# Feed-forward weight centred, scaled and summed on GpSimd beside the first softmax in a gated cross-attention block

## The chip, the cores and the metric

The kernel runs on one core of a Trainium2 chip. A core has five engines, each with an instruction queue that is worked off in order: TensorE (PE; its weight loads are listed as PEld), VectorE (DVE), ScalarE (ACT), GpSimd (POOL) and SyncE (SP, which here only issues DMA transfers). The metric is the device time of one execution in microseconds (us), the median over several runs.

## What is computed

Four sequences of 2048 tokens with 512 features attend to 77 context vectors with 16 heads, and pass through a feed-forward layer that is one matrix out of eight. Both branches are gated by the tanh of a scalar:

```python
q = split_heads(layernorm(x) @ Wq)
k, v = split_heads(context @ Wk), split_heads(context @ Wv)
attn = softmax(einsum('bhid,bhjd->bhij', q, k) * SCALE)
x = x + tanh(g_xattn) * (merge(einsum('bhij,bhjd->bhid', attn, v)) @ Wo + bo)
idx = argmax(log_softmax(logits) + gumbel(u))
x = x + tanh(g_ffn) * (layernorm(x) @ W[idx] + b[idx])
```

All of it is in fp32.

## The kernel before

**Tiling.** The 8192 tokens are worked off in 16 groups of 512. Weights are folded first: `m` holds `Wq` and the keys of one sequence in one matrix, `vo` holds values times `Wo` times the gate, `wf` holds the chosen feed-forward matrix, centred over its input features and times its gate `tgf`. A group is then three products: scores (`ps_s`, weight `m`), attention (`ps_a`, weight `vo`) and feed-forward (`ps_f`, weight `wf`).

**Seven products in place of eight.** Every product of 2x2 blocks is done with seven block products (class `Seven`, lines 440 to 491). It needs sums of blocks on both sides: `weight_sum(w, n)` (L119) forms the weight's, four of them, into blocks 5, 3, 4 and 6 of a tile with 7 blocks; `Columns.sum` (L429) forms `T1` to `T4` of the tokens, in the tile `tq`. In `ORDER` (L442) step `s` multiplies one block and accumulates it in one of three PSUM banks; `post(s)` (L477) takes the result out. Steps 0, 1, 2 and 6 are copies on ACT (L467), steps 3, 4 and 5 additions on VectorE (L486). Step 2 accumulates further in the bank of step 0, so its matmuls wait until `post(0)` has copied that bank; step 4 waits so for `post(2)`, step 6 for `post(4)`.

**Order.** The order on every engine is that of the program text, written out by hand; nothing reorders it. An instruction waits for the semaphores of what it reads or overwrites. PSUM is one pool of 7 banks, taken in turn.

**The start of the kernel,** where the change lies:

- Weights are folded on TensorE (`project_k`, `project_v`, `build_m`). `kT`, the keys, lies in the first 2560 columns of the tile `wf`, and the last of the values, `vT[7]`, in columns 2560 to 2879 (L256); both are done with before `wf` gets its own contents there. `build_vo(p)` (L322) multiplies a pair of heads' values with `Wo`, with two evictions for each third of the keys on VectorE (`D`) or ACT (`A`), and stores the result to DRAM; `load_vo` loads it back.
- The scores of group 0 come in three parts: `s0` and `s1` with two pairs of heads' rows each, `s2` with one (L669, L683, L712). While `s0` runs, `gather` (L242) fetches the rows of the feed-forward weight to the tile `wfr` by indirect DMA, and GpSimd adds its four pieces (`sum_wf`, L629) into `wf`'s first 512 columns.
- While `s1` runs (L684 to L709), VectorE takes the statistics of group 1 in four steps of four (`n1.stats`, L698). At step 4 `centre_wf` (L635) lets TensorE form the mean of the weight in PSUM (a matmul with `ones`), and VectorE subtracts it from the four pieces. At step 5 ACT gathers group 1's statistics with eight small copies (`n1.gather`, L374, placed as `norm_step(n1, 0)`), and `scale_wf` (L641) has ACT multiply by `tgf` and write `wf`'s blocks 0 to 3 in eight operations.
- While `s2` runs, VectorE computes group 1's variance (`n1.calc`, L376) and GpSimd raises it to the power -1/2 (L393, `n1.power`).
- Then the scores of group 1 run on TensorE, with `build_vo(4)` to `build_vo(7)` between their steps, beside the first softmax: `head_max` on VectorE, `exps` on ACT, `head_sum` on VectorE, `head_scale` (L542) on GpSimd, `p_columns` (the transposes to `pT`, L546) on VectorE.
- `weight_sum(wf, 0)` stands between the third and fourth `head_scale` of group 0, and `weight_sum(wf, 1..3)` in the first attention (L868 to L872). The first feed-forward follows at L911.

Of the kernel before, what the change touches and what calls it, by code (L numbers as in the profile page):

```python
# [10 lines left out]
AF = mybir.ActivationFunctionType  # L11
ALU = mybir.AluOpType
# [7 lines left out]
def flamingo_block_kernel(  # L20
# [33 lines left out]
    nc = tc.nc  # L54
    NT, D = x.shape
# [7 lines left out]
    NP = H // 2  # L63
# [6 lines left out]
    BP = B * JP  # L70
    NDC = D // P
# [16 lines left out]
    def bank(name):  # L88
        return pm.tile([P, 512], F32, tag="mm", name=name)
# [6 lines left out]
    BLK = {(0, 0): 0, (0, 1): 1, (1, 1): 2, (1, 0): 3}  # L96
    m = cp.tile([P, 7, 2, KH, P], F32, tag="m")
    vo = cp.tile([P, 7, KH, D // 2], F32, tag="vo")
    wf = cp.tile([P, 7, 2, D // 2], F32, tag="wf")
# [14 lines left out]
    def flat(t):  # L114
        n = len(t.shape) - 1
        names = " ".join("abcdef"[:n])
        return t.rearrange(f"p {names} -> p ({names})")

    def weight_sum(w, n, engine=None):  # L119

        to, a, b_, op = ((5, 0, 3, ALU.subtract), (3, 3, 2, ALU.add), (4, 3, 0, ALU.subtract),
                         (6, 1, 4, ALU.subtract))[n]
        (engine or nc.gpsimd).tensor_tensor(flat(w[:, to]), flat(w[:, a]), flat(w[:, b_]), op)  # L123

    m_f, vo_f, wf_f = flat(m), flat(vo), flat(wf)
# [17 lines left out]
    t = wp.tile([P, NK * T + KH * T2], F32, tag="pT", name="wq")  # L143
    wq_f = t[:, : NP * D]
    wq = wq_f.rearrange("p (n f) -> p n f", n=NP)
    vT_f = t[:, NP * D :]
    xg, ys, ts_ = {}, {}, {}
# [17 lines left out]
    for _ in range(3):  # L165
        ps = bank("ps_w")
# [22 lines left out]
    def by_chunk(t):  # L189

        return t.rearrange("p (a q e) -> p q a e", a=NA, e=32)

    def chunked(t):
        return t.rearrange("p (q a e) -> p q a e", a=NA, e=32)
# [3 lines left out]
    tgx, tgf = tg[:, 0:1], tg[:, 1:2]  # L198
# [43 lines left out]
    def gather():  # L242
        t = row_tile("wfr").rearrange("p g j -> p (g j)").rearrange("p (c d) -> p c d", c=NDC)
        for c in range(NDC):
            at = bass.IndirectOffsetOnAxis(ap=rows_u[:, c : c + 1], axis=0)
            nc.gpsimd.indirect_dma_start(out=t[:, c, :], out_offset=None, in_=W, in_offset=at)
        at = bass.IndirectOffsetOnAxis(ap=rows_u[:, NDC:], axis=0)
        nc.gpsimd.indirect_dma_start(out=bf_r, out_offset=None,
                                     in_=b.rearrange("o (a j) -> (o a) j", j=P), in_offset=at)
        nc.gpsimd.tensor_scalar(bo_c, bo_c, tgx, None, ALU.mult)  # L250
        nc.gpsimd.tensor_scalar(bf_r, bf_r, tgf, None, ALU.mult)
        return t


    kT = wf_f[:, : NP * BP].rearrange("p (n b k r) -> p n b k r", n=NP, b=B, r=R)
    vT = [(vT_f[:, ts(p, BP)] if p < 7 else wf_f[:, ds(NP * BP, BP)]).rearrange(  # L256
        "p (r b k) -> p r b k", b=B, r=R) for p in range(NP)]

    kT_f = kT.rearrange("p n b k r -> p n b (k r)")
# [252 lines left out]
    def s_rows(i, k, cols):  # L512
        if i not in sc:
            sc[i] = wp.tile([P, HA, NG, JP], F32, tag="s", name="s")
        nc.vector.transpose(key_chunk(sc[i], k), cols.rearrange("p (g h r) -> p g h r", h=HA, r=R))  # L515
# [6 lines left out]
    def head_max(i, h):  # L522
        mx = stat[:, ds((16 + h) * NG, NG)]
        nc.vector.tensor_reduce(mx, head(i, h), AX.X, ALU.max)  # L524
        nmx[h] = small.tile([P, NG], F32, tag=f"nmx{h}", name="nmx")
        nc.vector.tensor_tensor(nmx[h], mx, norms[i].down, ALU.mult)  # L526
# [102 lines left out]
    def sum_wf(wfr):  # L629
        t = wf_f[:, :D]  # L630
        nc.gpsimd.tensor_tensor(t, wfr[:, 0, :], wfr[:, 1, :], ALU.add)
        nc.gpsimd.tensor_tensor(t, t, wfr[:, 2, :], ALU.add)
        nc.gpsimd.tensor_tensor(t, t, wfr[:, 3, :], ALU.add)

    def centre_wf(wfr):  # L635
        ps = bank("ps_w")
        nc.tensor.matmul(ps, ones, wf_f[:, :D], start=True, stop=True)
        for c in range(NDC):
            nc.vector.tensor_tensor(wfr[:, c, :], wfr[:, c, :], ps, ALU.subtract)

    def scale_wf(wfr):  # L641
        for c in range(NDC):
            for o in range(2):
                nc.scalar.activation(chunked(wf[:, BLK[o, c // 2], c % 2, :]),  # L644
                                     by_chunk(wfr[:, c, :])[:, ts(o, 2)], AF.Copy, scale=tgf)

    def scores0(i):
        return Seven("ps_s", w_scores, xc[i], (0, 1), SNAP)
# [7 lines left out]
    def norm_step(n, s):  # L656
        if s == 0:
            n.gather()
        elif s == 1:
            n.calc()  # L660
            n.power()
        elif s == 2:
            n.back()
# [6 lines left out]
    for s in range(6):  # L670
        s0.product(s)
        if s == 0:
            gates2()
            wfr = gather()
# [9 lines left out]
    for s in range(7):  # L684
        s1.product(s)
        if s == 0:
            s1.post(0)
            s0.product(6)
            s0.post(6)
            norm_step(n, 0)  # L690
            for k in range(2):
                s_rows(0, KH + k, s0.chunk(1, k))
            sum_wf(wfr)
        elif s == 1:
            norm_step(n, 1)
        if 0 < s:
            s1.post(s)
        if 2 <= s < 6:  # L698
            n1.stats(xg[1], 0, 4 * (s - 2), 4)
        if s == 3:  # L700
            norm_step(n, 2)
        if s == 5:
            norm_step(n1, 0)
        if s == 4:
            centre_wf(wfr)
        if s == 5:
            scale_wf(wfr)
            for k in range(2):
                s_rows(0, 2 + k, s1.chunk(0, k))  # L709
    for k in range(2):  # L710
# [24 lines left out]
    for s in range(6):  # L735
        s0.product(s)
        s0.post(s)
        if s < 4:
            build_vo(4 + s, "DDA" if s < 2 else "D")
        if s < 2:  # L740
            head_max(0, 2 + s)
        exps(0, e[s], e[s + 1])
        if s == 3:
            load_vo(0)
        if 3 <= s:
            head_sum(0, s - 3)
            head_scale(0, s - 3)
    exps(0, 57, 64)
    for s in range(7):
        s1.product(s)  # L750
        s2.product(s)
        if s == 0:
            s1.post(0)
            s2.post(0)
            s0.product(6)
            s0.post(6)
            weight_sum(wf, 0)
            head_sum(0, 3)
            head_scale(0, 3)
        if s == 3:  # L760
            norm_step(n1, 2)
        if 1 <= s < 5:
            p_columns(0, (0, 2, 5, 7)[s - 1], (2, 5, 7, 10)[s - 1])
        if s == 2:
            pT[0].sum("T1")
        if s == 3:
            weight_sum(vo, 0)
        if s == 4:
            weight_sum(vo, 1)
        if s == 5:  # L770
            weight_sum(vo, 2)
            for k in range(4):
                s_rows(1, (0, 1, KH, KH + 1)[k], s0.chunk(k // 2, k % 2))
        if 0 < s:
            s1.post(s)
            s2.post(s)
# [5 lines left out]
    for i in range(1, NGRP):  # L782
# [69 lines left out]
        for s in range(7):  # L852
            at.product(s)
            if s == 0:
                pT[j].sum("T2")
                if 0 <= f:
                    f_scale(f, n.rs, 10, 6)
                    f_add(f, 0, NG, nc.gpsimd)
                    store(f)
                head_max(i, 0)  # L860
                head_max(i, 1)
            if s == 1:
                head_max(i, 2)
                head_max(i, 3)
            if 1 <= s:
                e = (0, 10, 20, 32, 44, 56, 64)
                exps(i, e[s - 1], e[s])
            if s == 0 and i == 1:  # L868
                pT[j].sum("T3")
                weight_sum(vo, 3)  # L870
                for t in range(1, 4):
                    weight_sum(wf, t)  # L872
            if s == 2:
                pT[j].sum("T4")
                if swap_m:
                    weight_sum(m, 0)
                if not last:
                    x_columns(nx)
                    norms[nx].stats(xg[nx], norms[nx].x0, 0, 8)
                head_sum(i, 0)  # L880
                head_scale(i, 0)
            if s == 3:
                if not last:
                    norms[nx].stats(xg[nx], norms[nx].x0, 8, 8)
                    if nx + 1 < NGRP:
                        load(nx + 1)
            if s == 4:
                residual(j, at, "11")
                head_sum(i, 1)
                head_scale(i, 1)  # L890
            if s == 5:
                head_sum(i, 2)
                head_scale(i, 2)
                residual(j, at, "22")
            if s == 6:
                residual(j, at, "12")
                residual_last(j, at)
                head_sum(i, 3)
            else:
                at.post(s)  # L900
# [37 lines left out]
    n1, n0 = Norms(NGRP + 1, NG // 2), Norms(NGRP + 2, NG // 2)  # L938
# [144 lines left out]
```

## Time and profile before

| what | value |
|---|---|
| median of 3 runs | 1262.63 us (1260.26 to 1262.82) |
| profiled execution | 1261.98 us |
| its span, first to last instruction | 1260.2 us |
| mean granted TensorE clock | 0.994 of full speed |
| ACT busy, share of the span | 54% |
| GpSimd busy, share of the span | 70% |
| TensorE's whole waiting on other engines, as its view of waits lists it | 8.6 us: 5.6 ACT `snap`, 1.5 start, 0.8 VectorE `sn`, 0.4 VectorE `snap`, 0.3 GpSimd `tq` |

How to read the profile: the page and its views come from one execution. "L461" is line 461 of the kernel. A row of the timeline is: start in us, duration in us, engine, line, operation, output <- inputs, partitions x elements, count; in brackets the idle time ahead of it and what ended it. In the timeline a matmul of fp32 counts as two records. PEclk is the granted TensorE clock as a share of full speed. A time that TensorE idles counts on the whole only if nothing later waits for something else anyway.

### The profile page before, as it was taken

To read this page: it belongs to the slowest core of one execution; us is meant where nothing else is said; L and a number is where in the kernel's file an instruction comes from. 1 tells how busy PE (TensorE), PEld (TensorE's weight loads), DVE (VectorE), ACT (ScalarE), POOL (GpSimd) and SP (SyncE) were. 2 spreads that over 40 slices of the span, in tenths; PEclk is the share of its full clock that TensorE was granted. 3 is DMA by queue.
4 is the path that set the end of the run, shared out by engine and by line. 5 is a ranking of instruction groups with operands and counts; after the bars stand their busy time and mean duration, and the time that the engine had idled before them with its cause. 6 is when DMAs were issued, how large, how long until landed. Compare 5 with 4: busy or idle time off the path is not lost.

```text
span 1260.2 us, 16984 instructions
## 1 busy us (share of the span) xinstructions
PE 1241.3 (99%) x5704; PEld 1061.0 (84%) x5704; DVE 914.0 (73%) x1859; ACT 685.6 (54%) x1964; POOL 876.8 (70%) x470
## 2 busy tenths in 40 slices
PE   9989999999999999999999999999999999999996
PEld 6665888888888888888888888888888888888885
DVE  5778876677776767777776877666777876666577
ACT  3547473827456483736548373654738274564823
POOL 4332896685967778584968778575986877585766
PEclk9999999999999999999999999999999999999998
DMA  9775500304006030303206030122304111010102
GB/s 254 293 214 179 147 1 1 68 21 116 15 1 151 1 68 1 67 1 93 58 1 151 1 67 1 26 42 84 67 1 109 43 43 25 1 34 1 34 1 67
DMA packets 95221, 80.27 MB, mean 64 GB/s; under 512 B 3856, under 2 KB 83088, under 8 KB 95136
## 3 DMA queue, kind: packets, MB, share of 16 engines
q1 hardware_dynamic: 92768, 76.74, 23.8%
q0 software_dynamic: 608, 1.13, 0.4%
q10 hardware_dynamic: 1760, 1.34, 0.3%
q8 instruction: 45, 0.74, 0.2%
q14 instruction: 40, 0.33, 0.1%
HBM read 44.07 MB, written 35.13 MB: 63 GB/s over the span
## 4 chain that ended last, share of the span: by engine, by line
PE 93%; POOL 3%; DVE 2%; ACT 1%; DMA 1%; issue 0%; SPq 0%; POOLq 0%; DVEq 0%; ACTq 0%
PE ps_s L461 36%; PE ps_a L461 36%; PE ps_f L461 15%; PE ps_kv L266 2%; PE ps_vo L331 2%; PE ps_m L296 2%; POOL vo L123 1%; DMA xg<-in_x_dram 1%; POOL pT L432 1%; PE ps_w L167 0%; POOL s L543 0%; DVE snap L486 0%; POOL xc L558 0%; ACT wf L644 0%; POOL wf L123 0%
## 5 line engine op out<-in xcount | busy, mean ns | idle before, releaser
L461 PE MATMUL ps_a<-pT,vo 128*128 128x256 f32 x2240 | 486.2, 379 | 0.0
L461 PEld LDWEIGHTS ps_a<-pT,vo 128*128 128x128 f32 x2240 | 425.6, 190 | 57.9
L532 ACT ACTIVATE s<-s,nmx,up 128x77 f32<-128x77 f32 x1024 | 355.6, 446 | 1.0 <-DVE nmx L526 1.0
L432 POOL TENSOR_TENSOR pT<-pT 128x1280 f32<-128x1280 f32 x64 | 185.8, 2905 | 171.5 <-PE ps_a L461 162.0
L461 PE MATMUL ps_s<-tq,m 128*128 128x256 f32 x1280 | 292.4, 381 | 6.5 <-ACT snap L467 5.6
L461 PEld LDWEIGHTS ps_s<-tq,m 128*128 128x128 f32 x1280 | 243.3, 191 | 43.9 <-ACT snap L467 6.4
L467 ACT COPY snap<-ps_s 128x512 f32<-128x512 f32 (+1 forms) x188 | 93.3, 514 | 289.2 <-DVE t L412 131.3
L461 PE MATMUL ps_s<-xc,m 128*128 128x256 f32 x960 | 222.3, 381 | 0.0
L461 PEld LDWEIGHTS ps_s<-xc,m 128*128 128x128 f32 x960 | 182.6, 191 | 29.3 <-DVE vo L334 2.4
L543 POOL TENSOR_TENSOR s<-s,sm 128x1232 f32<-128x1232 f32 x64 | 145.2, 2270 | 64.0 <-DVE sm L540 41.6
L486 DVE TENSOR_TENSOR snap<-snap,ps_s 128x512 f32<-128x512 f32 (+1 forms) x141 | 83.5, 593 | 123.5 <-PE ps_s L461 120.7
L461 PE MATMUL ps_f<-tq,wf 128*128 128x256 f32 x512 | 118.5, 379 | 0.6 <-DVE snap L486 0.4
L552 DVE STREAM_TRANSPOSE pT<-s 128x512 f32<-128x512 f32 x160 | 101.0, 678 | 18.2 <-POOL s L543 18.2
L393 POOL TENSOR_TENSOR r<-r,neghalf 32x16 f32<-32x16 f32 (+1 forms) x33 | 93.1, 2831 | 29.6 <-DVE r L388 29.1
L432 POOL TENSOR_TENSOR tq<-xc,tq 128x512 f32<-128x512 f32 x64 | 85.3, 1333 | 34.8 <-PE ps_f L461 32.3
L461 PEld LDWEIGHTS ps_f<-tq,wf 128*128 128x128 f32 x512 | 97.1, 190 | 14.5 <-issue 0.7
L515 DVE STREAM_TRANSPOSE s<-snap 128x512 f32<-128x512 f32 x156 | 99.8, 685 | 10.1 <-ACT snap L467 7.9
L539 DVE TENSOR_REDUCE sm<-s 128x16 f32<-128x1232 f32 x64 | 91.5, 1430 | 20.8 <-ACT s L532 20.7
L524 DVE TENSOR_REDUCE ps_st<-s 128x16 f32<-128x1232 f32 x64 | 92.4, 1444 | 2.1
L432 POOL TENSOR_TENSOR tq<-xc 128x512 f32<-128x512 f32 x64 | 81.4, 1272 | 13.7 <-DVE xc L407 12.3
L461 PE MATMUL ps_f<-xc,wf 128*128 128x256 f32 x384 | 90.7, 379 | 0.0
L467 ACT COPY snap<-ps_f 128x512 f32<-128x512 f32 x63 | 36.9, 585 | 88.9 <-PE ps_f L461 88.8
(126 smaller groups left out, 1180.3 us busy)
## 6 DMA issues: line engine op xcount, KB each, us to landing
xg<-in_x_dram SPq DMA_DIRECT2D x64, 256.0 KB, 6.2
out_dram<-y SPq DMA_DIRECT2D x60, 256.0 KB, 4.1
vo<-vo_d SPq DMA_DIRECT2D x16, 640.0 KB, 5.5
vo_d<-vo SPq DMA_DIRECT2D x16, 512.0 KB, 3.8
m<-m_d SPq DMA_DIRECT2D x12, 640.0 KB, 4.1
m_d<-vo SPq DMA_DIRECT2D x4, 960.0 KB, 6.1
wq<-in_WqT_dram SPq DMA_DIRECT2D x8, 256.0 KB, 8.0
wq<-in_Wo_dram SPq DMA_DIRECT2D x1, 2048.0 KB
```

The source lines that it names most:

```text
L266: nc.tensor.matmul(ps[:, :n], w[:, c, ts(p, P)], keys[:, c].rearrange("p b j -> p (b j)"), start=(c == 0), stop=(c == NCC - 1))
L393: nc.gpsimd.tensor_tensor(r, r, neghalf[:32, : r.shape[1]], ALU.pow)
L432: (engine or nc.gpsimd).tensor_tensor(self.at[name], self.at[a], self.at[b_], op)
L461: nc.tensor.matmul(self.ps[r][:, n, :], self.w(blk, c, pair), self.cols(cname, c), start=(first and n == 0 and c == 0), stop=(c == h - 1), ...
L467: nc.scalar.copy(dst, self.ps[r])
L486: nc.vector.tensor_tensor(c, c, self.ps[r], ALU.add)
L515: nc.vector.transpose(key_chunk(sc[i], k), cols.rearrange("p (g h r) -> p g h r", h=HA, r=R))
L524: nc.vector.tensor_reduce(mx, head(i, h), AX.X, ALU.max)
L532: nc.scalar.activation(head(i, h)[:, g, :], head(i, h)[:, g, :], AF.Exp, scale=norms[i].up[:, g : g + 1], bias=nmx[h][:, g : g + 1])
L539: nc.vector.tensor_reduce(sm, head(i, h), AX.X, ALU.add)
L543: nc.gpsimd.tensor_tensor(head(i, h), head(i, h), sums[h].unsqueeze(2).to_broadcast([P, NG, J]), ALU.mult)
L552: nc.vector.transpose(pT[i].all[:, k, :].rearrange("p (g h r) -> p g h r", h=HA, r=R), key_chunk(sc[i], k))
```

## The change

`wf` keeps the same contents, but is made at another time and by another engine. TensorE's matmul for the mean stays where it was, and ACT copies the mean from PSUM to `wf`'s block 5 (`mean_wf`). GpSimd then subtracts it and scales, one piece after the other (`centre_wf`), two pieces in each of the first two steps of group 1's first scores, behind the four `tq` sums of group 1 in its queue. The first two weight sums follow at step 2 and the third at step 3, ahead of the first `head_scale`; the fourth stays in the first attention. VectorE's four subtractions and ACT's eight scalings are gone. `vT[7]` moves from block 5 of `wf` to block 6. The statistics of group 1 are taken in steps 2, 3 and 4 of `s1` as 6, 6 and 4, instead of in four steps of 4.

```diff
-    vT = [(vT_f[:, ts(p, BP)] if p < 7 else wf_f[:, ds(NP * BP, BP)]).rearrange(
+    vT = [(vT_f[:, ts(p, BP)] if p < 7 else wf_f[:, ds(6 * D, BP)]).rearrange(
...
-    def centre_wf(wfr):
+    wf_mean = wf_f[:, ds(5 * D, D)]
+
+    def mean_wf():
         ps = bank("ps_w")
         nc.tensor.matmul(ps, ones, wf_f[:, :D], start=True, stop=True)
-        for c in range(NDC):
-            nc.vector.tensor_tensor(wfr[:, c, :], wfr[:, c, :], ps, ALU.subtract)
-
-    def scale_wf(wfr):
-        for c in range(NDC):
-            for o in range(2):
-                nc.scalar.activation(chunked(wf[:, BLK[o, c // 2], c % 2, :]),
-                                     by_chunk(wfr[:, c, :])[:, ts(o, 2)], AF.Copy, scale=tgf)
+        nc.scalar.copy(wf_mean, ps)
+
+    def centre_wf(wfr, c):
+        nc.gpsimd.tensor_tensor(wfr[:, c, :], wfr[:, c, :], wf_mean, ALU.subtract)
+        for o in range(2):
+            nc.gpsimd.tensor_scalar(chunked(wf[:, BLK[o, c // 2], c % 2, :]), by_chunk(wfr[:, c, :])[:, ts(o, 2)],
+                                    tgf, None, ALU.mult)
...
-        if 2 <= s < 6:
-            n1.stats(xg[1], 0, 4 * (s - 2), 4)
+        if 2 <= s < 5:
+            n1.stats(xg[1], 0, 6 * (s - 2), 4 if s == 4 else 6)
...
         if s == 4:
-            centre_wf(wfr)
+            mean_wf()
         if s == 5:
-            scale_wf(wfr)
             for k in range(2):
                 s_rows(0, 2 + k, s1.chunk(0, k))
...
         s0.post(s)
+        if s < 2:
+            centre_wf(wfr, 2 * s)
+            centre_wf(wfr, 2 * s + 1)
+        if s == 2:
+            weight_sum(wf, 0)
+            weight_sum(wf, 1)
+        if s == 3:
+            weight_sum(wf, 2)
         if s < 4:
             build_vo(4 + s, "DDA" if s < 2 else "D")
...
             s0.post(6)
-            weight_sum(wf, 0)
             head_sum(0, 3)
...
                 weight_sum(vo, 3)
-                for t in range(1, 4):
-                    weight_sum(wf, t)
+                weight_sum(wf, 3)
```

## The prediction

> **What bounds the kernel now.** I read four views in this order: the page's busy times, TensorE's waits, TensorE's timeline with the granted clock, and then the timelines of the engines that TensorE waits for.
>
> ```profile
> PE 1241.3 (99%) x5704; PEld 1061.0 (84%) x5704; DVE 914.0 (73%) x1859; ACT 685.6 (54%) x1964; POOL 876.8 (70%) x470
> ```
>
> TensorE (PE) is busy for all but 18.9 us of the span, so a change that leaves its matmuls alone can win only part of these 18.9 us, plus whatever matmuls run slowly. Where are the gaps? TensorE's waits from 90 to 240 us:
>
> ```profile
> PE ps_s L461 <- ACT snap L467: 5.3, 1, 5.3
> PE ps_s L461 <- DVE sn L486: 0.8, 1, 0.8
> PE ps_f L461 <- POOL tq L432: 0.3, 1, 0.3
> ```
>
> These three lie in or behind the stage that the change touches. TensorE's timeline round the largest (start, duration, releaser in brackets; each matmul is two records):
>
> ```profile
> 87.59 1.03 PE L461 MATMUL ps_s<-xc,m 128*128 128x256 f32 x4
> 88.46 1.03 PE L461 MATMUL ps_s<-tq,m 128*128 128x256 f32 x4
> 94.78 2.07 PE L461 MATMUL ps_s<-tq,m 128*128 128x256 f32 x4 [5.30 <-ACT snap L467]
> 96.64 1.91 PE L461 MATMUL ps_s<-xc,m 128*128 128x256 f32 x4
> 98.35 1.34 PE L461 MATMUL ps_s<-tq,m 128*128 128x256 f32 x4
> 99.53 1.03 PE L461 MATMUL ps_s<-xc,m 128*128 128x256 f32 x4
> ```
>
> These are the seven steps of `s2` of group 0. Start to start, a step takes 0.87 us ahead of the gap, but 1.86, 1.71 and 1.18 us behind it. The windows say why (length, then the busy time of PE, PEld, DVE, ACT, POOL, then PEclk):
>
> ```profile
> 95.00:97.00 2.00, 2.00 (x5) 1.62 (x6) 1.90 (x7) 0.11 (x1) 0.00 (x0) 0.50 0.00 0
> 97.00:99.00 2.00, 2.00 (x6) 1.57 (x5) 0.87 (x4) 0.26 (x1) 1.31 (x1) 0.50 0.00 0
> 99.00:101.00 2.00, 2.00 (x10) 1.70 (x10) 0.91 (x3) 0.00 (x0) 2.00 (x2) 1.00 0.00 0
> ```
>
> After the gap the clock is at half for some 4 us. So the gap costs more than 5.3 us: with 0.865 us a step, `s2`'s third step could begin at 87.59 + 2 x 0.865 = 89.32 and `s2` end at 93.65; it ends at 101.35 (when the next matmul of `build_vo` starts). That is 7.70 us, 5.46 of gap and 2.24 of slow clock.
>
> ACT in that time:
>
> ```profile
> 89.07 0.19 ACT L374 COPY ps_st<-s 32x32 f32<-32x32 f32 x1 [3.46 <-DVE s L365]
> ...
> 90.69 3.30 ACT L644 ACTIVATE wf<-wfr,tg 128x256 f32<-128x256 f32 x8
> 93.90 1.10 ACT L467 COPY snap<-ps_s 128x512 f32<-128x512 f32 x3
> ```
>
> Step 2 of `s2` accumulates in the bank that `s2.post(0)`, one of the three copies at 93.90, must empty first. Ahead of it stand ACT's eight gather copies of group 1 (1.62 us, waiting for VectorE's last statistics) and the eight scalings of the feed-forward weight (3.30 us).
>
> [...] a gap of 5.3 us, then clock 0.50 until about 99 us. [...] Here a 128x512 subtraction took 0.67 us on VectorE from PSUM (L639), and a 128x512 sum 1.27 us on GpSimd. [...]
>
> **The change, part by part.**
>
> *VectorE ahead of the gap.* Removed: four L639 subtractions, 2.38 us in the chain. The 16 statistics stay, in steps 2, 3, 4 as 6+6+4, at 0.197 us each. From the trace's 81.71: six (1.18) to 82.9, add of step 3 (0.6) to 83.5, six to 84.7, add of step 4 (0.6) to 85.3, four (0.8) to 86.1. Before, the last ended at about 88.9. The add of step 4 must be done before `s1`'s step 6 at 85.87: 0.5 us to spare.
>
> *ACT.* Added: one copy of the mean, 128x512 from PSUM, 0.55 us by L467's two in 1.07. Removed: 3.30 us. ACT ends the `rs` copies at 85.61 as before; mean copy to 86.2; gathers (1.62) to 87.8; `s1.post(6)` (0.55) to 88.35; `s2.post(0)` after its product, by about 89.0. TensorE wants it at 89.32, so the wait goes, with 0.3 us to spare. What is late next? VectorE: two transposes to 87.95, two to 89.65, `calc` (1.9 us in the trace) to 91.55, add of `s2`'s step 3 to 91.97, of step 4 to about 92.5; step 6 is due at 92.79. No gap, but margins of 0.3 us. **Gain: 7.70 us.** Nothing else moves on TensorE: its queue is unchanged.
>
> *GpSimd.* Its `pow` for group 1 starts when `calc` ends, 91.5 in place of 97.69, and takes 2.9; the four sums of `xc[1]` take 5.1, to 99.5. Then come the moved operations: four subtractions at 1.27 (5.1), eight scalings 128x256, and three of the four weight sums at 1.27 (3.8). The scaling has a twin, same shape and same strided source, in the first stage:
>
> ```profile
> L289 POOL TENSOR_SCALAR wqp<-wq,wqm 128x256 f32<-128x256 f32 x8 | 8.7, 1082 | 10.3 <-DVE wqm L284 9.7
> ```
>
> 8 x 1.08 = 8.7. Sum 17.5 us, to 117.0. Where does it fit?
>
> ```profile
> 104.38 1.27 POOL L432 TENSOR_TENSOR tq<-xc,tq 128x512 f32<-128x512 f32 x1
> 127.85 6.72 POOL L543 TENSOR_TENSOR s<-s,sm 128x1232 f32<-128x1232 f32 x3 [22.20 <-issue]
> 134.52 1.26 POOL L123 TENSOR_TENSOR wf<-wf 128x512 f32<-128x512 f32 x1
> 135.75 2.27 POOL L543 TENSOR_TENSOR s<-s,sm 128x1232 f32<-128x1232 f32 x1
> ```
>
> GpSimd is idle for 22.2 us here, until the first head is to be scaled. With everything 7.7 us earlier that head is due at 120.15, so 3.1 us stay free: the 17.5 us cost nothing. I take 1.08 us each; the lower bound is 0.6 (L251, 128x128 and half the size), the upper one I leave open to 1.5[...]. At 1.5 the work ends at 120.4, 0.2 us late.
>
> *Behind it.* The weight sum at 134.52 leaves the chain head scaling, then VectorE's transposes to `pT` (which idle 4.17 us for GpSimd's last scaling), then the additions that TensorE waits 0.81 us for at 145.65. All this comes 1.26 us earlier against TensorE: the 0.81 us go, 0.45 to spare. **Gain: 0.81 us.** Of the three sums at 161.95 (3.97 us) two are gone; the exponentials of group 1 start up to 1.26 - 0.81 = 0.45 us earlier against TensorE, since VectorE's maxima release them, and with them the residuals and the first `tq` sum that feed-forward waits 0.26 us for. **Gain: 0.26 us.**
>
> *Placement.* `vT[7]` moves to block 6 so that the mean can lie in block 5; no instruction is added, and `build_vo(7)` gains no wait on GpSimd. The load of group 3 gains one, for reads that end by 113, before its issue (131.97 - 7.7 = 124.3). Cost nothing.
>
> Sum: 7.70 + 0.81 + 0.26 = 8.77 us. After group 1's first feed-forward TensorE waited 0.4 us in all until the tail, so the whole gain should reach the end. Span 1260.2 - 8.8 = 1251.4; the profiled execution took 1261.98, 1.8 more, giving 1253.2. The median shown is 0.65 us above that execution, which would give 1253.9. I take 1253.5.
>
> **Rivals.**
> *A shorter gap stays.* If the gathers start no earlier than before (89.07), ACT goes on to 89.07 + 1.62 + 0.55 + 0.37 = 91.6 and TensorE waits 2.3 us, [...] gain 7.70 - 2.3 + 1.07 = 6.5, time 1256. For it: margins of 0.3 us on both engines. Against: the statistics have no wait left that could delay them.
> *GpSimd becomes the bound, and the kernel is slower.* If the strided scalings take much longer beside VectorE, the head scaling is late and TensorE waits for the first attention. It decides per scaling: from 1.08 + (3.1 + 0.45)/8 = 1.52 us TensorE begins to wait; from 1.52 + 8.77/8 = 2.6 us all is lost; at 3.0 the time would be about 1265. For it: L289 ran in a quieter stage. Against: [...] GpSimd's 128x512 sums took 1.27 us in the busy stages too.
> *The gain is lost at the first attention.* The transfer of `vo` (5.6 us from issue to landing) or the exponentials could hold it at its old time. But every store that it waits for is issued by evictions that start 7.7 us earlier, and the first sum of `vo` waited for no transfer. If half were lost: 1258.
>
> **How the numbers follow.** Forecast 0.82 (1252 to 1255.5); shorter gap 0.08; lost at the attention, in part to wholly, 0.06; GpSimd slower 0.04. A change under 0.2% (2.5 us) can't be told from none by this kernel's runs, which spread from 1260.26 to 1262.82. Faster: 0.82 + 0.08 + 0.03 = 0.93; the same 0.04; slower 0.03. The range reaches from 1251.8, where every gap of this stretch is gone and the run is a quick one, up to 1257, past the shorter gap.
>
> **What would show it.** Right: no wait of TensorE on ACT near 89 us, clock 1.0 from 89 to 101, `s2` ended near 93.7, the twelve new GpSimd operations and three sums between 99 and 118, the first head scaled near 120, the waits of 0.8 and 0.3 us gone. Wrong: gathers that start after 87 us, scalings above 1.5 us each, or a new wait of TensorE between 110 and 175 us.

## The result, and the profile after

The changed kernel takes 1254.14 us in the median (1252.23 to 1254.62), beside 1262.32 us of the kernel before (1260.26 to 1262.82; four runs now, with the three of the table above among them) on the same chip: a ratio of 0.9932, with a 95% interval of 0.992 to 0.9944. The forecast was 1253.5 us. The profiled execution took 1252.23 us, with a span of 1250.3.

TensorE's waits over the whole span, of the changed kernel (us in total, times, longest):

```profile
PE ps_w L167 <- DVE tq L163: 1.5, 1, 1.5
PE ps_f L461 <- DVE snap L486: 0.4, 1, 0.4
PE ps_s L461 <- ACT snap L467: 0.3, 1, 0.3
```

All three waits that the prediction quoted are gone; the 0.3 us left on ACT's `snap` is an older wait, near 77 us. The first line is the start, the second the tail. `s2` of group 0 in TensorE's timeline:

```profile
86.64 1.03 PE L461 MATMUL ps_s<-xc,m 128*128 128x256 f32 x4
87.51 1.89 PE L461 MATMUL ps_s<-tq,m 128*128 128x256 f32 x8
89.23 1.03 PE L461 MATMUL ps_s<-xc,m 128*128 128x256 f32 x4
90.10 1.03 PE L461 MATMUL ps_s<-tq,m 128*128 128x256 f32 x4
90.96 1.03 PE L461 MATMUL ps_s<-xc,m 128*128 128x256 f32 x4
91.82 1.03 PE L461 MATMUL ps_s<-tq,m 128*128 128x256 f32 x4
```

The row with x8 is two steps that merge because nothing lies between them. From one start to the next, the first six steps take 0.87 us each and the last, ahead of `build_vo(3)`, 0.96. The windows of the same stretch (length, busy PE, PEld, DVE, ACT, POOL, then PEclk) show the clock at 1.00 where it was 0.50:

```profile
95.00:97.00 2.00, 2.00 (x10) 1.17 (x7) 1.90 (x4) 1.96 (x4) 2.00 (x2) 1.00 0.00 0
97.00:99.00 2.00, 2.00 (x10) 0.96 (x10) 1.83 (x4) 1.99 (x5) 2.00 (x3) 1.00 0.81 283
```

ACT's queue, where the gap was made:

```profile
84.69 0.58 ACT L640 COPY wf<-ps_w 128x512 f32<-128x512 f32 x1
85.17 0.19 ACT L374 COPY ps_st<-s 32x32 f32<-32x32 f32 x1
...
86.84 0.58 ACT L467 COPY snap<-ps_s 128x512 f32<-128x512 f32 x1
87.71 0.37 ACT L467 COPY snap<-ps_s 128x256 f32<-128x256 f32 x1 [0.28 <-PE ps_s L461]
```

ACT now waits for TensorE at the copy of 87.71 and not the other way round. The copy ends at 88.08, and TensorE's third step is due at 87.51 + 0.86 = 88.37: 0.3 us to spare. GpSimd's moved work:

```profile
98.58 1.27 POOL L643 TENSOR_TENSOR wfr<-wfr,wf 128x512 f32<-128x512 f32 x1
99.94 1.83 POOL L645 TENSOR_SCALAR wf<-wfr,tg 128x256 f32<-128x256 f32 x2
...
111.20 3.97 POOL L123 TENSOR_TENSOR wf<-wf 128x512 f32<-128x512 f32 x3
119.27 8.94 POOL L543 TENSOR_TENSOR s<-s,sm 128x1232 f32<-128x1232 f32 x4 [4.10 <-DVE sm L540]
```

It ends at 115.2, and 4.10 us of idle time remain ahead of the head scaling, whose four now run without a sum between them.

A span compares badly across executions, because the start-up varies. It is better cut at starts of TensorE's rows:

| stretch of TensorE's queue | before | after | less |
|---|---|---|---|
| start to the mean's matmul (`ps_w`) | 83.28 | 82.33 | 0.95 |
| to `build_vo(3)`, that is the end of `s2` | 18.07 | 10.45 | 7.62 |
| to the first attention | 47.00 | 45.91 | 1.09 |
| to step 1 of the first feed-forward | 32.36 | 32.20 | 0.16 |
| to the last block of matmuls | 1067.21 | 1067.19 | 0.02 |
| to the end of the span | 12.28 | 12.22 | 0.06 |

The first row does not belong to the change: TensorE's program up to there is the same. In the traces of the experiments below this start is anywhere from 82.49 to 84.71 us, and both ends of that range belong to executions of one and the same program, so it is scatter, and part of why single runs of one kernel spread over some 2 us. The next three rows, 8.87 us together, are the change's. They agree with the ratio (0.0068 of 1262.3 is 8.6 us), and the fifth row shows that nothing is given back in the rest of the kernel.

### The profile page after: what moved, and what is told of

It reads as the page before. It is cut to its first block, busy times and chain, and to the rows that moved or that the text cites. A ratio compares the mean times of both kernels' runs of the same rounds, so it can differ in the third digit from the quotient of the medians.

```text
span 1250.3 us, 16985 instructions
## 1 busy us (share of the span) xinstructions
PE 1237.8 (99%) x5704; PEld 1059.4 (85%) x5704; DVE 911.6 (73%) x1855; ACT 683.0 (55%) x1957; POOL 888.9 (71%) x482
## 4 chain that ended last, share of the span: by engine, by line
PE 94%; DVE 3%; ACT 1%; POOL 1%; issue 0%; DVEq 0%; ACTq 0%; POOLq 0%
PE ps_s L461 37%; PE ps_a L461 36%; PE ps_f L461 15%; PE ps_kv L266 2%; PE ps_vo L331 2%; PE ps_m L296 2%; ACT s L532 1%; POOL s L543 1%; DVE s L515 1%; DVE pT L552 0%; PE ps_w L167 0%; DVE snap L486 0%; DVE t L412 0%; DVE vo L334 0%; DVE sm L539 0%
## 5 line engine op out<-in xcount | busy, mean ns | idle before, releaser
L539 DVE TENSOR_REDUCE sm<-s 128x16 f32<-128x1232 f32 x64 | 91.5, 1429 | 20.7 <-ACT s L532 20.6
```

What stands on the lines that cost most here:

```text
L539: nc.vector.tensor_reduce(sm, head(i, h), AX.X, ALU.add)
```

## The experiments

Each is read by its time and by the same stretches: A is the mean's matmul to `build_vo(3)`, B from there to the first attention, C to step 1 of the first feed-forward. A stretch comes from one profiled execution. A ratio is to runs of the kernel before that were made alongside (their medians lie between 1262.3 and 1262.8 us), so it isn't exactly the quotient of the medians shown.

| kernel | median, us | ratio to before (95%) | A | B | C |
|---|---|---|---|---|---|
| before | 1262.32 | | 18.07 | 47.00 | 32.36 |
| changed | 1254.14 | 0.9932 (0.992 to 0.9944) | 10.45 | 45.91 | 32.20 |
| statistics alone | 1257.61 | 0.9967 (0.9954 to 0.9979) | 13.15 | 46.98 | 32.34 |
| changed, statistics as before | 1253.91 | 0.9935 (0.9922 to 0.9947) | 11.29 | 45.91 | 32.18 |
| changed, sums back | 1254.58 | 0.994 (0.9927 to 0.9953) | 10.45 | 46.99 | 32.34 |
| before, gap filled with matmuls, first trial | 1262.34 | 1.0 (0.9992 to 1.0008) | 17.60 | 46.98 | 32.36 |
| before, gap filled with matmuls, second trial | 1260.25 | 0.9982 (0.9975 to 0.9988) | 16.13 | 47.00 | 32.34 |
| before, ACT's scalings later | 1255.48 | 0.9946 (0.9932 to 0.996) | 11.82 | 46.98 | 32.36 |
| changed, 4 scalings twice | 1254.31 | 0.9936 (0.992 to 0.9951) | 10.45 | 45.91 | 32.19 |
| changed, 8 scalings twice | 1257.64 | 0.9963 (0.995 to 0.9976) | 10.45 | 50.07 | 32.39 |

**One part alone: the statistics.**

```diff
-        if 2 <= s < 6:
-            n1.stats(xg[1], 0, 4 * (s - 2), 4)
+        if 2 <= s < 5:
+            n1.stats(xg[1], 0, 6 * (s - 2), 4 if s == 4 else 6)
```

> The kernel before with one part of the change: group 1's statistics as 6, 6 and 4 in steps 2 to 4, all else as before. Theory (ACT's queue ahead of s2's first copy sets the gap[...]): the statistics end at about 86, the gathers start near 86 in place of 89, then the scalings, then the copies, s2's step 2 starts near 92 in place of 94.8. Gap about 2.8 us, clock 1.00 all through, time 1257.4 (5 us less than before). Rival (the statistics are hidden, the eight scalings alone make the gap): no change, 1262.3, and the clock still falls to 0.50.

Measured: 1257.61 us. ACT and TensorE of this kernel:

```profile
86.93 3.31 ACT L644 ACTIVATE wf<-wfr,tg 128x256 f32<-128x256 f32 x8
90.14 1.09 ACT L467 COPY snap<-ps_s 128x512 f32<-128x512 f32 x3
```

```profile
91.02 1.13 PE L461 MATMUL ps_s<-tq,m 128*128 128x256 f32 x4 [2.33 <-ACT snap L467]
91.99 1.03 PE L461 MATMUL ps_s<-xc,m 128*128 128x256 f32 x4
```

The copy comes some 3 us earlier than in the kernel before, the wait is 2.33 us and the next step takes 0.97 us: the clock held in this execution (PEclk 1.00 from 87 to 101 us). Two changed lines and no moved work bring 4.92 us of stretch A here, and 3.49 in an execution in which the clock did not hold (below). The rival, that the statistics are hidden, falls.

**The rest alone.** The reverse: the changed kernel with the statistics in four steps of four.

```diff
-        if 2 <= s < 5:
-            n1.stats(xg[1], 0, 6 * (s - 2), 4 if s == 4 else 6)
+        if 2 <= s < 6:
+            n1.stats(xg[1], 0, 4 * (s - 2), 4)
```

> The changed kernel with the statistics in four steps of 4 again; centring, scaling and sums stay on GpSimd. Theory: the last four statistics wait behind the addition of s1's step 5, end near 87.4, the gathers follow, s2's step 2 starts some 0.7 us late, clock 1.00: 1254.8, and 0.5 to 0.9 us of wait of TensorE on ACT. Rival (the statistics are hidden): 1254.1, no wait. Rival 2 (the statistics carry most of the gain): 1259 or more.

Measured: 1253.91 us, with a wait at `s2`'s third step that is just under the 0.5 to 0.9 us expected:

```profile
89.68 1.13 PE L461 MATMUL ps_s<-tq,m 128*128 128x256 f32 x4 [0.47 <-ACT snap L467]
```

Stretch A is 0.84 us longer than in the changed kernel. The trace shows the cost that was expected; the time, 0.9935 (0.9922 to 0.9947), can't show 0.8 us. The two parts bring 4.92 and 6.78 us of A alone but 7.62 together: each shortens the same wait, and neither the wait nor the loss of clock behind it can be saved twice.

**The weight sums.**

```diff
-        if s == 2:
-            weight_sum(wf, 0)
-            weight_sum(wf, 1)
-        if s == 3:
-            weight_sum(wf, 2)
...
+            weight_sum(wf, 0)
             head_sum(0, 3)
...
-                weight_sum(wf, 3)
+                for t in range(1, 4):
+                    weight_sum(wf, t)
```

> The changed kernel with the three weight sums put back where they were: one between the third and fourth head scaling of group 0, two in the first attention. Theory: the sum delays the fourth scaling and so VectorE's transposes to pT by 1.26 us, TensorE's wait on VectorE near 136 us comes back (0.8 to 1.0 us), and the wait of the feed-forward on the first tq sum (0.3 us); time 1255.2. Rival (the wait near 145 us of the kernel before came from the gap ahead of it and goes with it): 1254.1 and no such wait.

Measured: 1254.58 us (expected 1255.2). That is 0.4 us above the changed kernel, which the times can't tell from none; the trace can. GpSimd has the sum between the scalings again, and TensorE two of its waits:

```profile
127.15 1.27 POOL L123 TENSOR_TENSOR wf<-wf 128x512 f32<-128x512 f32 x1
128.38 2.27 POOL L543 TENSOR_TENSOR s<-s,sm 128x1232 f32<-128x1232 f32 x1
```

```profile
138.28 2.86 PE L461 MATMUL ps_s<-tq,m 128*128 128x256 f32 x12 [0.82 <-DVE sn L486]
...
173.31 3.72 PE L461 MATMUL ps_f<-tq,wf 128*128 128x256 f32 x16 [0.23 <-POOL tq L432]
```

Stretch B is 46.99 again and C 32.34: 1.08 + 0.14 us. So, with the gap at `s2` gone as in the changed kernel, one sum of 1.27 us in the wrong place of a queue costs TensorE 1.1 us. The wait of the kernel before at 145 us came from this placement and not from the gap ahead of it.

**The clock.** A first trial put five matmuls into the gap that read `wf`:

```diff
     for s in range(7):
+        if s == 2:
+            ps = bank("ps_x")
+            for _ in range(5):
+                nc.tensor.matmul(ps, ones, wf_f[:, :D], start=True, stop=True)
         s2.product(s)
```

> The kernel before with five added matmuls of 128x512 between s2's steps 1 and 2, into a bank of their own, their result unused; they run while TensorE would idle. Theory: they take 5 x 0.87 = 4.3 us of the 5.5 us gap, so the copy releases step 2 at the same moment, but the clock stays at 1.00 and s2's last steps take 0.87 us each: 2.2 us less, 1260.1. Rival (the slow steps behind the gap have another cause, as late additions or copies): 1262.3 with steps of 1.2 to 1.9 us again.

It told little: 1262.34 us. The added matmuls read a block that ACT's scalings write, so they waited 2.59 us for them, and then stood in the way of `s2`'s third step, which began at 96.44:

```profile
92.04 4.56 PE L717 MATMUL ps_x<-wf,ones 128*128 128x512 f32 x10 [2.59 <-ACT wf L644]
96.44 1.03 PE L461 MATMUL ps_s<-tq,m 128*128 128x256 f32 x4
```

The steps behind it took 0.86 us, as expected, but nearly all that this saved was spent: stretch A is only 0.47 us shorter. The second trial read `m_f[:, :D]` instead:

> The kernel before with five added matmuls between s2's steps 1 and 2, result unused, now reading the weight m, which no engine writes then (the first trial read wf, and so waited for ACT's scalings). Theory: they start at once, end about 1.1 us before ACT's copy, step 2 starts near 94.8 as in the kernel before, the clock stays at 1.00 and the last steps of s2 take 0.87 us each: from the mean's matmul to build_vo 15.8 us in place of 18.1, time 1260.1. Rival (the slow steps have another cause): 18.1 us and 1262.3.

```profile
90.73 4.46 PE L717 MATMUL ps_x<-m,ones 128*128 128x512 f32 x10
96.20 1.13 PE L461 MATMUL ps_s<-tq,m 128*128 128x256 f32 x4 [1.01 <-ACT snap L467]
97.17 1.03 PE L461 MATMUL ps_s<-xc,m 128*128 128x256 f32 x4
98.03 1.03 PE L461 MATMUL ps_s<-tq,m 128*128 128x256 f32 x4
```

Measured: 1260.25 us (expected 1260.1), stretch A 16.13, that is 1.94 us shorter, though TensorE was released no earlier: from the mean's matmul to `s2`'s third step it is 11.51 us here and 11.50 in the kernel before. Nothing but the added matmuls differs between the two kernels. PEclk is 1.00 from 89 to 101 us here, where it was 0.50 from 93 to 98 us in the kernel before. So the slow steps behind the gap were the clock, and they cost about 2 us of the 7.62.

**Place in the queue or engine?** ACT keeps the scalings, behind its copy of `s2`'s step 2; VectorE keeps the centring; the statistics go 6, 6, 4.

```diff
         if s == 5:
-            scale_wf(wfr)
             for k in range(2):
...
         s2.product(s)
         s2.post(s)
         if s == 2:
+            scale_wf(wfr)
             norm_step(n1, 1)
```

> The kernel before with the statistics as 6, 6 and 4, and ACT's eight scalings placed behind its copy of s2's step 2, where ACT is idle; VectorE still centres, ACT still scales, and the weight sums stand where they stood. Theory (the place in ACT's queue made the gap, not the engine): no wait of TensorE near 89 us, clock 1.00, s2 ends near 93 to 94; the wait of 0.8 to 1.0 us on VectorE behind the fourth head scaling and the 0.3 us at the feed-forward stay: 1255.2. Rival (VectorE's centring holds the path too): a wait of 1 us or more near 89 us, 1256.5 or more.

Measured: 1255.48 us. ACT holds nothing up any more, but a new wait stands at `s2`'s last step, on VectorE:

```profile
94.86 1.13 PE L461 MATMUL ps_s<-tq,m 128*128 128x256 f32 x4 [1.10 <-DVE snap L486]
```

```profile
86.75 2.45 DVE L639 TENSOR_TENSOR wfr<-wfr,ps_w 128x512 f32<-128x512 f32 x4
...
94.05 1.08 DVE L486 TENSOR_TENSOR snap<-snap,ps_s 128x256 f32<-128x256 f32 x3
```

Here the theory was off in one point: it expected no wait at all, and the rival, that VectorE's centring holds the path too, came about in part, with a wait of the size it named at a later step. The four subtractions (2.45 us) push VectorE's transposes and `calc` back, and the additions of `s2`'s steps 3 to 5 come late. The place in ACT's queue, with the statistics, is worth 18.07 - 11.82 = 6.25 us of A; with the centring off VectorE it is 1.37 more. For ACT's part, then, the place is enough. For VectorE's part these runs don't tell place from engine: the centring at a later place in VectorE's own queue was not tried, and neither was a kernel with it and ACT's scalings both placed later, which might need no move to GpSimd at all.

**How much room GpSimd has.** The changed kernel with scalings done twice, four of them and then all eight:

```diff
-        for o in range(2):
+        for o in (0, 1, 1):
```

> The changed kernel with four of GpSimd's eight scalings done twice (same result): 4 x 0.92 = 3.7 us more. GpSimd idled 4.1 us ahead of the first head scaling. Theory (the moved work is hidden in that idle time): the idle time falls to 0.4 us, head scaling starts as before, time 1254.1. Rival (GpSimd's work beside the softmax already slows VectorE or sets the time): about 1257.

Measured: 1254.31 us, all stretches those of the changed kernel to 0.01 us. In GpSimd's timeline the head scaling follows the sums without idle time; the 0.4 us that should have been left are used up, since three scalings in a row take 2.84 us beside 1.82 of two, so an added one 1.02 and not 0.92:

```profile
117.37 3.98 POOL L123 TENSOR_TENSOR wf<-wf 128x512 f32<-128x512 f32 x3
121.38 8.94 POOL L543 TENSOR_TENSOR s<-s,sm 128x1232 f32<-128x1232 f32 x4
```

```diff
-        for o in range(2):
+        for o in (0, 1, 0, 1):
```

> The changed kernel with all eight scalings done twice: 8 x 0.92 = 7.4 us more, 3.3 us past the idle time. Theory: the first head scaling starts 3.3 us late, the transposes to pT as well, and TensorE waits near 136 us for VectorE, less 0.35 us that its addition had to spare: a wait of about 2.9 us, time 1257.2, the granted clock still 1.00. Rival (head scaling has slack elsewhere): 1254.1.

Measured: 1257.64 us, 0.4 us over what was expected. The wait is there, but stretch B is 4.16 us longer, not 2.9:

```profile
139.76 4.14 PE L461 MATMUL ps_s<-tq,m 128*128 128x256 f32 x12 [2.66 <-DVE sn L486]
143.69 2.56 PE L461 MATMUL ps_a<-pT,vo 128*128 128x256 f32 x9
```

```profile
140.00:141.00 1.00, 1.00 (x6) 0.87 (x6) 1.00 (x3) 0.00 (x0) 1.00 (x1) 1.00 0.00 0
141.00:142.00 1.00, 1.00 (x5) 0.80 (x4) 1.00 (x3) 0.00 (x0) 0.92 (x2) 0.59 0.00 0
142.00:143.00 1.00, 1.00 (x4) 0.82 (x3) 1.00 (x3) 0.58 (x1) 1.00 (x1) 0.50 0.00 0
```

From the start of the step with the wait to the next, 3.93 us passed here: the clock fell to half, and did so more than 1 us after TensorE had gone back to work. A wait of 2.33 us had cost no clock in the kernel with the statistics alone. Both kernels were profiled once more:

> A second look at the changed kernel with all eight scalings done twice, where a wait of 2.66 us was followed by half clock from about 1.5 us after work had resumed. If a wait of this length always costs the clock: half clock again, and 3.9 us for the six matmuls of the seventh step. [...] the same wait of 2.7 us, and either outcome; clock held, the six take 2.7 us.

> A second look at the kernel before with the statistics alone changed, where a wait of 2.33 us cost no clock. If waits of 2.3 us never cost the clock: 1.00 again and steps of 0.87 us. [...] the clock may fall here, and s2's later steps then take up to 1.8 us.

Both came out the other way round (one execution each, 1257.91 us and 1259.93 us). With the scalings twice, the wait was 2.67 us and the clock held (PEclk 1.00 from 137 to 146 us), so that the same step took 2.70 us:

```profile
141.19 2.86 PE L461 MATMUL ps_s<-tq,m 128*128 128x256 f32 x12 [2.67 <-DVE sn L486]
143.89 30.38 PE L461 MATMUL ps_a<-pT,vo 128*128 128x256 f32 x140
```

Stretch B was 48.85 us there, 2.94 more than in the changed kernel, as expected. In the first profile the first head scaling started 3.07 us later, counted from the mean's matmul (40.01 us in place of 36.94): beyond GpSimd's idle time, added work costs TensorE nearly one for one.

With the statistics alone, the wait was 2.33 us as before, and the clock fell (PEclk 0.50 from 93 to 96 us):

```profile
93.24 2.08 PE L461 MATMUL ps_s<-tq,m 128*128 128x256 f32 x4 [2.33 <-ACT snap L467]
95.11 1.66 PE L461 MATMUL ps_s<-xc,m 128*128 128x256 f32 x4
96.61 1.03 PE L461 MATMUL ps_s<-tq,m 128*128 128x256 f32 x4
```

Stretch A was 14.58 us there, 1.43 more than in the other execution of the same program. With the 2.59 us of the first filled gap, whose PEclk stayed at 1.00, five profiled executions had a wait of 2.3 to 2.7 us: the clock fell in two and held in three.

## Why the prediction was right, point by point

- *The gap and its slow clock, 7.70 us:* measured 7.62. The 0.08 us lie in the last step, which was priced at 0.865 us like the others and takes 0.96. The split into 5.46 of gap and 2.24 of clock is borne out to within 0.3 us by the filled gap, which saved 1.94 with the release where it was. That TensorE would be held by neither ACT nor VectorE is what the trace shows: ACT's copy ends at 88.08, 0.3 us ahead of the step due at 88.37, and VectorE itself waits 0.31 us for TensorE ahead of its addition of step 4 at 91.23.
- *The head scaling's weight sum, 0.81 us:* measured 1.09 in the changed kernel, and 1.08 lost again with the sums put back. The mechanism was right and the term too small: the wait as listed is only the idle part. In the kernel before, the step ahead of it took 3.56 us start to start in place of 2.59 (0.97 more), and the step with the wait 2.70 (0.11 more):

```profile
142.09 2.75 PE L461 MATMUL ps_s<-xc,m 128*128 128x256 f32 x12
145.65 2.86 PE L461 MATMUL ps_s<-tq,m 128*128 128x256 f32 x12 [0.81 <-DVE sn L486]
148.35 30.38 PE L461 MATMUL ps_a<-pT,vo 128*128 128x256 f32 x140
```

- *The first `tq` sum, 0.26 us:* measured 0.16. Step 0 of that feed-forward takes 1.98 us to the next start, where 1.73 would do, so GpSimd is still just late there (its `tq` sum runs until 170.84, the step starts at 170.89); the prediction took the wait as gone.
- *GpSimd, 17.5 us into 20.6:* the eight scalings took 0.92 us each, not the 1.08 of their twin row, and 4.1 us stayed free in place of 3.1. The four added scalings show that this room is real, the eight that TensorE waits once it is used up (2.66 us).
- *VectorE beside GpSimd's new work:* no slowing seen. VectorE's maxima over 128x1232 took 1.43 us with GpSimd idle beside them (105.59 in the kernel before) and 1.43 with GpSimd's new work beside them (101.43 in the changed one). Other operations were not compared.
- *The rivals.* None came about. The shorter gap as it was priced, 2.3 us, is what the statistics alone leave by another way, and there its one assumption failed: the gain of 6.5 us took the clock as holding behind such a wait, which no trace had shown. In one of two executions with a wait of 2.33 us it held, in the other PEclk was 0.50 from 93 to 96 us. Of the forecast's own sum nothing rests on it.
- *Trace against median:* 8.77 us were forecast; the three stretches give 8.87, the medians 8.2 and the ratio 8.6. That the sum came so close owes something to luck: its terms were off by 0.08 too much, 0.28 too little and 0.10 too much, and these errors in part cancel. The profiled execution of the changed kernel started up 0.95 us faster than that of the kernel before, which flatters its span and isn't the change's.

## What to carry to other kernels

When one engine is busy nearly all the time, look for its few gaps and ask what stands ahead of the releasing instruction in *its* queue; here reordering alone, with the statistics earlier on VectorE and the scalings later on ACT, brought 6.25 of the 8.87 us, each operation still on its old engine. Work moved to another engine was free here up to that engine's idle time ahead of its next due instruction (4.1 us), and cost nearly one for one beyond (3.07 us late, 2.94 us lost), so measure that idle time and move small sums with it that stand in the middle of a chain. Count the loss of clock behind a gap (1.5 to 2.2 us where it fell here), and don't rely on a gap of 2.3 us being short enough; between the kernel's start and its tail, waits of up to 1.1 us cost no clock in these traces, and none between 1.1 and 2.3 us was seen.

## What the hardware showed that I had not expected

A wait of TensorE of 2.33 us was followed by half clock in one of two profiled executions of the same program, and one of 2.66 us likewise, there setting in more than 1 us after the work had resumed. How often this happens can't be told from so few.

How long the half clock lasted can be estimated from the windows. The windows beside a switch show 1.00 or 0.50, and PEclk of a window with a switch in it is taken as their mean over time. Each pair of lines has the window of the fall and that of the return. The kernel before:

```profile
92.00:93.00 1.00, 0.00 (x0) 0.00 (x0) 0.00 (x0) 1.00 (x3) 0.00 (x0) 0.58 0.00 0
98.00:99.00 1.00, 1.00 (x4) 0.82 (x3) 0.33 (x1) 0.00 (x0) 1.00 (x1) 0.51 0.00 0
```

The statistics alone, second profile:

```profile
89.00:95.00 6.00, 3.67 (x13) 2.82 (x13) 4.70 (x11) 4.45 (x12) 0.00 (x0) 0.83 0.00 0
96.00:97.00 1.00, 1.00 (x5) 0.86 (x4) 0.19 (x2) 0.00 (x0) 0.84 (x1) 0.81 0.00 0
```

The scalings twice, first profile:

```profile
141.00:142.00 1.00, 1.00 (x5) 0.80 (x4) 1.00 (x3) 0.00 (x0) 0.92 (x2) 0.59 0.00 0
144.00:145.00 1.00, 1.00 (x4) 0.78 (x4) 1.00 (x2) 0.30 (x1) 0.92 (x2) 0.70 0.00 0
```

By this estimate the clock was at half from about 92.16 to 98.98, from 92.96 to 96.38 and from 141.18 to 144.60: 6.8, 3.4 and 3.4 us, behind waits of 5.30, 2.33 and 2.66 us. It fell 2.7, 2.0 and 4.1 us after the last matmul ahead of the wait had ended. So the slow stretch was as long behind 2.33 us as behind 2.66, and among the waits of 2.3 to 2.7 us the length did not decide whether the clock fell. What decided it was not shown.

The price can be estimated from this. At PEclk 0.50 a step of `s2` took 1.87 us (93.24 to 95.11 in the second profile of the statistics alone), where the same step took 0.97 at 1.00 (91.02 to 91.99 in the first), so about half of the time that TensorE works in the slow stretch is lost. With the statistics alone that is (96.38 - 93.24) / 2 = 1.6 us, and the two slow steps took 1.54 us more than in the other execution. With the scalings twice it is 1.7 us: 1.23 in the step with the wait and 0.46 in the attention behind it (30.67 us up to the feed-forward in place of 30.21). In the kernel before it is (98.98 - 94.78) / 2 = 2.1 us, beside the 1.94 that the filled gap saved.
